# Layer 0 of a two-layer transformer kernel: when x is loaded, where averages and band products are emitted, and where the chain matmuls queue

## The chip, the cores and the metric

The kernel runs on one core of a Trainium2 chip. The metric is device microseconds of one execution. The kernel before took a median of 3630.38 us in three runs (3630.13 to 3631.83).

The engines are named as in the profile: PE is TensorE (matmuls, with weight loads as PEld), DVE is VectorE, ACT is ScalarE, POOL is GpSimd, and SP is SyncE, whose queue issues nearly all DMAs.

## The reference, cut to what matters

The input is `x` of 16 batches x 512 tokens x 128 channels. Layer 0 adds half of a feed-forward network, then an attention, then half of the same network again. Layer 1 (experts around a linear attention) follows; the change doesn't touch it.

```python
x = x + 0.5 * _L0_ffn_ref(_layernorm(x), w_gate, w_up, w_down)
x = x + _L0_attn_ref(_layernorm(x), W_qkv, b_qkv, W_out, b_out, rel_emb_k, rel_emb_v)
x = x + 0.5 * _L0_ffn_ref(_layernorm(x), w_gate, w_up, w_down)

# _L0_ffn_ref: every linear quantizes its input and its weights to FP4 in blocks of 16
h = silu(fp4_linear(x, w_gate)) * fp4_linear(x, w_up)      # 128 -> 352
return fp4_linear(h, w_down)                               # 352 -> 128

# _L0_attn_ref: 16 heads of 8 channels, 512 queries and keys, relative positions clipped at 64
score = einsum('bhqd,bhkd->bhqk', q, k) + einsum('bhqd,qkd->bhqk', q, pe_k)
attn = softmax(score)
ctx = einsum('bhqk,bhkd->bhqd', attn, v) + einsum('bhqk,qkd->bhqd', attn, pe_v)
```

## The kernel before, in words

**Units.** Layer 0 works in 32 units: 16 batches, each in two halves of 256 queries. Unit `u = 2b + h` is half `h` of batch `b`. A unit has eight blocks of 32 queries (`bb`) and four key tiles of 128 (`kt`), so 32 score tiles of 128 keys x 512 (16 heads x 32 queries).

**Scores twice.** A score tile (`scores`, L263 and L267) is 4 matmuls of keys against queries, and 8 more with relative positions where the block lies near the diagonal ("in band"). It goes into one of three PSUM banks (`sps`, pool `pS`). `maxima` makes all 32 tiles of a unit once to find each query's maximum: VectorE reduces each tile (L341), then two reductions (L347), a transpose on TensorE (L349), and a write to DRAM and back (L353, L355) put the negative maximum into a row of the query tile `BD`. `main` makes the same tiles again, with the maximum subtracted; ScalarE takes the exponential (L369) into `PT`, one tile of 128 x 16 x 256 per key tile, in a pool of three buffers.

**Averages and band part.** After the eight scores of a key tile, `main` emits 16 matmuls `av<-PT,a_V` (averages of the values and the sum of weights, in two PSUM banks). After the last key tile that a group of four blocks needs, it emits the products with the relative value embeddings (`rps<-PT,a_TV`, 64 columns each) in two portions of two blocks, and four copies to `RV` (L403). Both go through `run` (L272, L274), which keeps a portion's matmuls together. At the unit's end `RV` goes to DRAM (`RD`, L406) and comes back in another layout as `a_cr` (L409), and ScalarE copies the averages to `cx` (L412).

**The chain around it.** Per batch and half there are `head` (the first feed-forward network, `FFN.half`), `fin` (L422 adds `a_cr` to `cx`; then transposes L430, division, transposes L437, copy L438, output projection L440, residual) and `tail` (the second network and the store of `x`, L486). Per batch there are `prep` (layer norm, query and key projections, split into two 16-bit parts, 22 DMAs to DRAM: `QS`, `QM`, `KSd`) and `prepV` (values, with adds at L321). `loads` reads the DRAM copies into `a_KS` (two buffers), `a_BD` and `a_TQ` (three buffers each, L315, L329, L330). Tiles of `x` have five buffers; `xload` (L475) fills one on SP's queue at the start of the batch's `head`.

**What sets the order.** Each of these is a Python generator, and a `yield` ends a portion. `interleave` gives each generator a number of portions `n` and a window from `f` to `t` in units, and always emits next the portion whose planned time `f + (t-f)*done/n` is least. The window constants are in `W`: before, `fin` of unit u runs at u+1.45 to u+1.9, its tail in the unit after that, `prep` of batch b+2 at 0 to 0.7 of the even unit 2b, and the head of batch b+3 at -0.1 to 1. Maxima run ahead of `main` by one unit less 14 portions; the 17th portion of a unit's maxima emits the loads of the next unit.

The framework then lays out each engine's queue at build time from a simulated timeline: of the instructions that are ready in it, the one emitted first goes next, so a later one may pass an earlier one that isn't ready. On the chip each engine works its queue strictly in this order. `issue_after(ins)` adds an order edge: what is traced inside is queued behind `ins` on the same engine; it doesn't wait for `ins` to finish.

Before the units, a prologue loads the weights, runs the heads of batches 0, 1 and 2, prep of batches 0 and 1, and the maxima of unit 0 with the first 14 portions of those of unit 1.

Of the kernel before, what the change touches and what calls it, by code (L numbers as in the profile page):

```python
# [8 lines left out]
F32 = mybir.dt.float32  # L9
# [16 lines left out]
class K:  # L26
# [23 lines left out]
    def ln_steps(s, xb, out, wk, n):  # L50
# [12 lines left out]
        yield  # L63
    def quant_steps(s, X, wk, P, nb, tag):

# [18 lines left out]
class FFN:  # L84
# [22 lines left out]
    def half(f, xb, half, wk, pp):  # L107
# [7 lines left out]
        for j in range(2): nc.tensor.transpose(ps[:,j*128:(j+1)*128],xq[:,j*128:(j+1)*128],s.ident)  # L115
        xqT=wk.tile([128,256],F32,name="f_x"); nc.scalar.copy(xqT,ps[:,:256]); yield
        h=wk.tile([128,2,I],F32,name="f_h")
        for j in range(2):
            t=h[:,j,:]
            g=pp.tile([128,512],F32,name="mps")  # L120
            nc.tensor.matmul(g[:,:I],xqT[:,j*128:(j+1)*128],f.wguT[:,0,:],start=True,stop=True)
# [3 lines left out]
            nc.tensor.matmul(u[:,:I],xqT[:,j*128:(j+1)*128],f.wguT[:,1,:],start=True,stop=True)  # L125
# [3 lines left out]
        for j in range(2):  # L129
            ps=pp.tile([128,512],F32,name="mps")  # L130
            for c in range(3):
                P=min(128,I-c*128)
                nc.tensor.transpose(ps[:P,c*128:(c+1)*128],hq[:,j,c*128:c*128+P],s.ident)
            hT=wk.tile([128,3,128],F32,name="hT",bufs=1)
            nc.scalar.copy(hT[:,0:2,:],ps[:,:256])
            nc.scalar.copy(hT[:96,2,:],ps[:96,256:384])  # L136
            for c in range(3):
                P=min(128,I-c*128)
                nc.tensor.matmul(ps[:,384:512],hT[:P,c,:],f.wdT[:P,c,:],start=(c==0),stop=(c==2),skip_group_check=True)  # L139
            nc.vector.scalar_tensor_tensor(xh[:,j,:],ps[:,384:512],0.5,xh[:,j,:],ALU.mult,ALU.add); yield  # L140
# [5 lines left out]
class Attn0:  # L146
# [110 lines left out]
    def scores(a, out, kt, half, b, BD, TQ, KS):  # L257
# [4 lines left out]
        for g in range(4):  # L262
            nc.tensor.matmul(o4[:,g],KS[:,sd,g*512+kt*128:g*512+(kt+1)*128],BD[:,g,:,b*32:b*32+32].rearrange("p h (x j) -> p x h j",j=4),start=(g==0),stop=(not ib and g==3),skip_group_check=True)  # L263
        if ib:
            for x in range(8):
                w0=kt*128-blk*32-x+a.OFF
                nc.tensor.matmul(out[:,x*64:x*64+64],a.ET[:,w0:w0+128],TQ[:,:,b*32+4*x:b*32+4*x+4],start=False,stop=(x==7),skip_group_check=True)  # L267

    xnT={}; pend={}; last=None
# [5 lines left out]
    def prep(a, b, xb, wk, pM):  # L275
# [6 lines left out]
        for j in range(4): nc.tensor.transpose(ps[:,j*128:(j+1)*128],xn[:,j,:],a.ident)  # L282
        xnT=a.xnT[b]=wk.tile([128,512],F32,name="xnT",bufs=2); nc.scalar.copy(xnT,ps); yield
        for z in range(2):
            ps=pM.tile([128,512],F32,name="mps")
            nc.tensor.matmul(ps,a.w[:,z*128:(z+1)*128],xnT,start=True,stop=True)
# [18 lines left out]
        nc.tensor.matmul(ps[:32],a.eb.rearrange("p a b -> p (a b)"),q,start=True,stop=True)  # L305
# [26 lines left out]
    def maxima(a, b, half, wk, pS, pM):  # L332
# [13 lines left out]
        for hh in range(2):  # L346
            nc.vector.tensor_reduce(mk[:,hh],mx.rearrange("p k (x s) b -> p s b x k",s=2)[:,hh],axis=AX.X,op=ALU.max)  # L347
        ps=pS.tile([128,512],F32,name="sps")
        nc.tensor.transpose(ps[:,:128],mk.rearrange("p s b x -> p (s b x)"),a.ident)  # L349
# [8 lines left out]
    def main(a, b, half, X, wk, big, pS, pA, pM):  # L358
        s=a.s; nc=a.nc; i=b%2
        u=(2*b+half)%3; BD=a.BD[u]; TQ=a.TQ[u]; KS=a.KS[b%2]; V=a.V[b%2]; RD=a.RD[half]; cr=a.cr[0]  # L360
        av=[pA.tile([128,512],F32,name=f"av{z}") for z in range(2)]
        RV=wk.tile([128,4,4,4,16],F32,name="RV")
        PT=[None]*4
        for kt in range(4):
            pt=big.tile([128,16,256],F32,name="PT"); PT[kt]=pt
            for bb in range(8):
                ps=pS.tile([128,512],F32,name="sps")
                a.scores(ps,kt,half,bb,BD,TQ,KS)
                nc.scalar.activation(pt[:,:,bb*32:bb*32+32].rearrange("p h (x j) -> p x h j",j=4),ps.rearrange("p (x h j) -> p x h j",x=8,j=4),AF.Exp)  # L369
                yield  # L370
            vs=a.vers(kt,half)
            mms=[]
            for z in range(4):
                for cg in range(4):
                    h=z*4+cg
                    o=av[z//2][cg*32:cg*32+32,(z%2)*256:(z%2)*256+256]
                    fs=(kt==0 and z%2==0)
                    mms.append(((o,V[:,2*kt-1+vs,h*9:h*9+32],pt[:,h,:]),dict(start=fs,stop=(kt==3),skip_group_check=True,tile_position=(0,cg*32))))
            a.run(mms)
# [658 lines left out]
```

## Time and profile before

| | |
|---|---|
| median of three runs | 3630.38 us |
| profiled execution | 3633.94 us, its span 3632.2 us |
| PE busy in the span | 2825.0 us (78%) |
| DVE, ACT, POOL busy | 2444.9, 1693.8, 838.9 us |
| mean granted TensorE clock | 0.900 |
| exps of layer 0 (L369) | from 175.5 to 1974.5 us, 1024 of 0.60 us |
| reduces of the maxima (L341) | from 126.4 to 1921.8 us, 1024 of 0.70 us |
| `x` loads (L475) | 16, the last issued at 1569.6 us |

A slice of the page's second part is 90.8 us, a digit is busy tenths. In a list of waits, a line names the engine and line that waited, what ended the wait, the total in us, the number of waits and the longest. In a table of stretches, each engine has its busy us and its instructions in brackets; then come the mean granted clock, the DMA engines' busy share and GB/s.

### The profile page before, as it was taken

The numbers are of one execution on the slowest core, as the hardware profiler recorded it, in microseconds if no ns is written. First come the engines' busy times: TensorE is split into PE (matmuls) and PEld (weight loads), VectorE is DVE, ScalarE is ACT, GpSimd is POOL, SyncE is SP. The second block draws the span as 40 slices with busy tenths as digits, with TensorE's granted clock in tenths as the row PEclk, the third lists the DMA queues.
The fourth block names the chain that finished last, engine by engine and source line by source line (L and its number), as shares of the span: only waits on it lengthen the run. The fifth ranks groups of instructions, "written<-read, shape, count | busy, mean of one in ns | idle before, by whom it ended". The sixth has DMA issues, their size and how long they took to land. (4 is left out here: it accounts for less than half of the span.)

```text
span 3632.2 us, 95259 instructions
## 1 busy us (share of the span) xinstructions
PE 2825.0 (78%) x40077; PEld 2032.3 (56%) x40077; DVE 2444.9 (67%) x6508; ACT 1693.8 (47%) x3391; POOL 838.9 (23%) x789
## 2 busy tenths in 40 slices
PE   5578989889898889888896388873788888878570
PEld 3357777667676677666775244431565555555230
DVE  5568788777887788877773467774546655655356
ACT  3145555545455454545554155533455454445242
POOL 4122222222222222222110222212112211111226
PEclk8799999999999999999998599886899989989785
DMA  3232222321223222222210111104312222121401
GB/s 105 54 91 71 57 53 59 81 63 52 65 65 77 64 50 58 76 74 62 53 33 19 32 33 36 36 33 123 90 54 73 59 63 56 36 62 36 126 17 46
DMA packets 290159, 217.23 MB, mean 60 GB/s; under 512 B 77402, under 2 KB 257476, under 8 KB 289604
## 3 DMA queue, kind: packets, MB, share of 16 engines
q1 hardware_dynamic: 284468, 207.72, 21.6%
q8 instruction: 315, 5.16, 0.6%
q10 hardware_dynamic: 5264, 3.43, 0.4%
q14 instruction: 112, 0.92, 0.1%
HBM read 110.28 MB, written 100.78 MB: 58 GB/s over the span
## 5 line engine op out<-in xcount | busy, mean ns | idle before, releaser
L341 DVE TRANSPOSE_TENSOR_REDUCE mx<-sps 128x16 f32<-128x512 f32 x1024 | 702.5, 701 | 261.7 <-PE sps L263 137.2
L263 PE MATMUL sps<-a_BD,a_KS 128*128 128x128 f16 x8192 | 736.4, 222 | 136.2 <-DVE mx L341 65.6
L369 ACT ACTIVATE PT<-sps 128x512 f32<-128x512 f32 x1024 | 576.4, 599 | 433.8 <-PE sps L267 238.1
L263 PEld LDWEIGHTS <-a_KS 128*128 128x128 f16 x8192 | 546.1, 98 | 296.4 <-issue 260.0
L59 POOL TENSOR_TENSOR ln_rs<-ln_ve,negh 128x4 f32<-128x4 f32 (+1 forms) x192 | 176.9, 930 | 855.1 <-DVE ln_ve L58 760.6
L267 PE MATMUL sps<-a_TQ,a_ET 128*128 128x64 f16 x7168 | 370.3, 195 | 0.0
L721 DVE SCALAR_TENSOR_TENSOR moe<-mps,oh,moe 128x128 f32<-128x128 f32 x896 | 289.8, 341 | 110.7 <-PE mps L719 96.5
L79 POOL TENSOR_TENSOR q_M<-q_y,q_M 128x704 f32<-128x704 f32 (+2 forms) x129 | 157.0, 1218 | 784.6 <-DVE q_y L78 658.6
L719 PE MATMUL mps<-f_W,T 128*128 128x512 f32 x512 | 297.1, 701 | 24.8 <-DVE moe L721 20.0
L267 PEld LDWEIGHTS <-a_ET 128*128 128x128 f16 x7168 | 311.2, 99 | 2.3 <-issue 1.9
L274 PE MATMUL av<-PT,a_V 128*32 128x256 f32 x3840 | 251.9, 387 | 0.0
L894 DVE TENSOR_TENSOR a_at<-pp,a_cm 128x1024 f32<-128x1024 f32 x128 | 154.3, 1214 | 79.6 <-PE pp L892 78.6
L892 PE MATMUL pp<-a_F 64*128 64x128 f32 x2048 | 169.8, 306 | 41.4 <-DVE a_at L894 30.2
L892 PEld LDWEIGHTS pp<-a_F 64*128 64x128 f32 x2048 | 143.3, 206 | 93.0 <-DVE a_at L894 36.9
L719 PEld LDWEIGHTS mps<-f_W,T 128*128 128x128 f32 x512 | 102.7, 222 | 125.0 <-issue 75.3
L274 PEld LDWEIGHTS av<-PT,a_V 128*32 128x32 f32 x3840 | 121.4, 111 | 68.7 <-issue 5.0
L874 ACT ACTIVATE a_F<-pp 128x1024 f32<-128x1024 f32 x128 | 127.0, 1025 | 46.8 <-PE pp L872 40.5
L62 ACT ACTIVATE xn<-xn,ln_mr,ln_rs 128x128 f32<-128x128 f32 x256 | 103.6, 481 | 95.5 <-DVE ln_mr L60 75.2
L274 PE MATMUL rps<-PT,a_TV 128*32 128x64 f32 x6912 | 134.5, 222 | 4.6 <-issue 4.4
L139 PE MATMUL mps<-wdT,hT 128*128 128x128 f32 (+1 forms) x768 | 126.9, 301 | 5.6 <-ACT hT L136 4.0
L673 ACT COPY f_PT<-St 32x512 f32<-32x512 f32 x128 | 78.7, 615 | 106.0 <-DVE St L672 99.9
L872 PE MATMUL pp<-a_QK,a_PK 128*128 128x512 f16 x256 | 82.7, 413 | 54.4 <-DMA a_QK<-a1d 26.6
(342 smaller groups left out, 5330.2 us busy)
## 6 DMA issues: line engine op xcount, KB each, us to landing
QM<-a_HM SPq DMA_DIRECT2D x180, 128.0 KB
a_TQ<-QM SPq DMA_DIRECT2D x120, 192.0 KB
RD<-RV SPq DMA_DIRECT2D x32, 512.0 KB
a_KS<-KSd SPq DMA_DIRECT2D x128, 96.0 KB
a_QK<-a1d SPq DMA_DIRECT2D x128, 96.0 KB
xn<-X SPq DMA_DIRECT2D x32, 256.0 KB
a1d<-a_hi SPq DMA_DIRECT2D x64, 128.0 KB
a_BD<-QS SPq DMA_DIRECT2D x128, 58.0 KB
```

The lines of the kernel that those rows point to most:

```text
L59: nc.gpsimd.tensor_tensor(rs,ve,s.negh[:,:n],ALU.pow); yield
L79: nc.gpsimd.tensor_tensor(M[:P],y[:P],M[:P],ALU.subtract)
L263: nc.tensor.matmul(o4[:,g],KS[:,sd,g*512+kt*128:g*512+(kt+1)*128],BD[:,g,:,b*32:b*32+32].rearrange("p h (x j) -> p x h j",j=4),start=(g==0 ...
L267: nc.tensor.matmul(out[:,x*64:x*64+64],a.ET[:,w0:w0+128],TQ[:,:,b*32+4*x:b*32+4*x+4],start=False,stop=(x==7),skip_group_check=True)
L274: for p,q in mms[1:]: a.nc.tensor.matmul(*p,**q)
L341: with a.s.tc.high_priority(): r=nc.vector.tensor_reduce(mx[:,kt,:,bb],ps.rearrange("p (i c) -> p i c",c=32),axis=AX.X,op=ALU.max,apply_tr ...
L369: nc.scalar.activation(pt[:,:,bb*32:bb*32+32].rearrange("p h (x j) -> p x h j",j=4),ps.rearrange("p (x h j) -> p x h j",x=8,j=4),AF.Exp)
L719: nc.tensor.matmul(ps,yT[:,j*128:(j+1)*128],a.W[:,e2*4:e2*4+4,:],start=True,stop=True)
L721: nc.vector.scalar_tensor_tensor(moe[:,j,:],ps[:,e*128:(e+1)*128],oh[:,j,e2*4+e:e2*4+e+1],moe[:,j,:],ALU.mult,ALU.add)
L874: nc.scalar.activation(f,ps,AF.Relu)
L892: nc.tensor.matmul(ps[:,hh,bs],f[hh*64:hh*64+64,1,bs],f[hh*64:hh*64+64,0,bs],start=True,stop=True)
L894: nc.vector.tensor_tensor(k,ps.rearrange("p h (b q) -> p (h b) q",b=4),a.cm.unsqueeze(1).to_broadcast([128,8,128]),ALU.mult)
```

## The change

- `x` of batches 3 and later is loaded by a generator of its own, `xl`, through ScalarE's queue, with a window 1.4 to 1.3 units ahead of unit 2b where b+2 is the batch; `head` no longer loads.
- Heads run for batch b+2 (`hl` 2 for 3) in the window -1.05 to 0, `prep` at 1.03 to 1.9, `fin` at 0.6 to 1.0; the head of batch 2 leaves the prologue. Windows are cut at 0 below and 0.5 above.
- `main` yields after each score and nowhere else (32 portions for 59). Averages, band portions and copies are put on a list `todo`; after each score's exp one of them is taken off and emitted, so that those of a key tile come among the scores of the next one, and a unit's last ones among the next unit's first scores. What is left at the end is emitted by `rest`.
- `scores` remembers its last matmul in `lastmm`. The matmuls of `half`, `prep` (not `prepV`), `fin` and the transpose in `maxima` are traced inside `gate`, an `issue_after` of it.
- New yields: between `hT` and the down projection (L136/L139), before the transpose in `maxima` (L349), and between `ct` and the output projection (L438/L440).

```diff
+    lastmm=None
+    def gate(s):
+        return s.tc.issue_after(s.lastmm) if s.lastmm is not None else ExitStack()
...
     def half(f, xb, half, wk, pp):
...
-        for j in range(2): nc.tensor.transpose(ps[:,j*128:(j+1)*128],xq[:,j*128:(j+1)*128],s.ident)
+        with s.gate():
+            for j in range(2): nc.tensor.transpose(ps[:,j*128:(j+1)*128],xq[:,j*128:(j+1)*128],s.ident)
...
             hT=wk.tile([128,3,128],F32,name="hT",bufs=1)
             nc.scalar.copy(hT[:,0:2,:],ps[:,:256])
-            nc.scalar.copy(hT[:96,2,:],ps[:96,256:384])
+            nc.scalar.copy(hT[:96,2,:],ps[:96,256:384]); yield
             for c in range(3):
                 P=min(128,I-c*128)
-                nc.tensor.matmul(ps[:,384:512],hT[:P,c,:],f.wdT[:P,c,:],...)
+                with s.gate(): nc.tensor.matmul(ps[:,384:512],hT[:P,c,:],f.wdT[:P,c,:],...)
...
     def scores(a, out, kt, half, b, BD, TQ, KS):
...
+        a.s.lastmm=getattr(r,"ins",r)
...
     def maxima(a, b, half, wk, pS, pM):
...
+        yield
         ps=pS.tile([128,512],F32,name="sps")
-        nc.tensor.transpose(ps[:,:128],mk.rearrange("p s b x -> p (s b x)"),a.ident)
+        with a.s.gate(): nc.tensor.transpose(ps[:,:128],mk.rearrange("p s b x -> p (s b x)"),a.ident)
...
     def main(a, b, half, X, wk, big, pS, pA, pM):
...
+        PT=[None]*4; T={}; vers=a.vers
+        def avrun(kt):
+            if kt==0: T["av"]=[pA.tile([128,512],F32,name=f"av{z}") for z in range(2)]
+            vs=vers(kt,half)
+            mms=[]
+            for z in range(4):
+                for cg in range(4):
+                    h=z*4+cg
+                    o=T["av"][z//2][cg*32:cg*32+32,(z%2)*256:(z%2)*256+256]
+                    fs=(kt==0 and z%2==0)
+                    mms.append(((o,V[:,2*kt-1+vs,h*9:h*9+32],PT[kt][:,h,:]),dict(start=fs,stop=(kt==3),skip_group_check=True,tile_position=(0,cg*32))))
+            a.run(mms)
+        def rvrun(hb, b0, ks):
+            if b0%4==0: T["rps"]=pA.tile([128,512],F32,name="rps"); T["first"]=[True]*4
+            rps=T["rps"]; first=T["first"]
+            mms=[]
+            ok=[(bb,k) for k in reversed(ks) for bb in (b0+1,b0) if a.inband(k,half*8+bb)]
+            for bb,k in ok:
+                blk=half*8+bb
+                for x in range(8):
+                    cg=x%4; col=(bb-hb*4)*128+(x//4)*64
+                    v0=(blk*32-k*128+a.UO)//8-8*vers(k,half)
+                    mms.append(((rps[cg*32:cg*32+32,col:col+64],a.TV[vers(k,half)][:,x,v0:v0+4,:].rearrange("p v d -> p (v d)"),
+                        PT[k][:,:,bb*32+4*x:bb*32+4*x+4]),
+                        dict(start=first[cg],stop=(k==min(q for p,q in ok if p==bb)),skip_group_check=True,tile_position=(0,cg*32))))
+                    first[cg]=False
+            a.run(mms)
+        def rvcopy(hb):
+            if hb==0: T["RV"]=wk.tile([128,4,4,4,16],F32,name="RV")
+            for c in range(4):
+                nc.scalar.copy(T["RV"][:,:,c,:,hb*8:hb*8+8].rearrange("p j z a -> p a z j"),T["rps"].rearrange("p (a z c j) -> p c a z j",a=8,z=4,j=4)[:,c])
+        def end():
+
+            nc.sync.dma_start(RD[:,:4*8*1024].rearrange("x (r f) -> x r f",f=1024),T["RV"])
+            for c in range(4):
+                src=bass.AP(tensor=RD.tensor,offset=RD.offset+c*64,ap=[[1024,8],[8*1024+256,16],[1,64]])
+                nc.sync.dma_start(cr[c*32:c*32+8].rearrange("p (xj f) -> p xj f",f=64),src)
+            cx=wk.tile([128,4,256],F32,name="cx")
+            for zz in range(2):
+                nc.scalar.copy(cx[:,2*zz:2*zz+2,:].rearrange("p z (b j x) -> p (z b) x j",j=4,x=8),T["av"][zz].rearrange("p (y x j) -> p y x j",x=8,j=4))
+            a.pend[b,half]=cx,cr
         for kt in range(4):
             pt=big.tile([128,16,256],F32,name="PT"); PT[kt]=pt
             for bb in range(8):
                 ps=pS.tile([128,512],F32,name="sps")
                 a.scores(ps,kt,half,bb,BD,TQ,KS)
                 nc.scalar.activation(pt[:,:,bb*32:bb*32+32]...,AF.Exp)
+                if a.todo: a.todo.pop(0)()
                 yield
-            a.run(mms)
-            for _ in range(4): yield
+            a.todo.append(lambda kt=kt: avrun(kt))
             for hb in range(2):
                 bl=range(hb*4,hb*4+4)
                 ks=[k for k in range(4) if any(a.inband(k,half*8+x) for x in bl)]
                 if max(ks)!=kt: continue
...
+                a.todo+=[lambda hb=hb,b0=b0,ks=ks: rvrun(hb,b0,ks) for b0 in bl[::2]]+[lambda hb=hb: rvcopy(hb)]
+            if kt==3: a.todo.append(end)
+    def rest(a):
+        while a.todo: a.todo.pop(0)(); yield
...
     def fin(a, b, half, X, wk, pM):
...
-        ct=wk.tile(...); nc.scalar.copy(ct,ps[:,:256])
+        ct=wk.tile(...); nc.scalar.copy(ct,ps[:,:256]); yield
         ps=pM.tile([128,512],F32,name="mps")
-        for t in range(2): nc.tensor.matmul(ps[:,t*128:(t+1)*128],ct[:,t*128:(t+1)*128],a.wo,start=True,stop=True)
+        with s.gate():
+            for t in range(2): nc.tensor.matmul(ps[:,t*128:(t+1)*128],ct[:,t*128:(t+1)*128],a.wo,start=True,stop=True)
...
-        def xload(b):
-            if b in X or b>=nb: return
+        def xload(b, eng=nc.sync):
             t=xk.tile([128,4,128],F32,name="x"); X[b]=t
-            nc.sync.dma_start(t,tok(src,b))
+            eng.dma_start(t,tok(src,b))
+        def xl(b):
+            xload(b,nc.scalar); yield
         def head(b,h):
-            if b<nb: xload(b); yield from F.half(X[b],h,fk,pF)
+            if b<nb: yield from F.half(X[b],h,fk,pF)
...
-        pl,hl=2,3
-        W=dict(part=0,V=(.6,.7),fin=(.45,.9),prep=(0,.7),tail=1.0,head=(-.1,1))
+        pl,hl=2,2
+        W=dict(part=0,V=(.6,.7),fin=(.6,1.0),prep=(1.03,1.9),tail=1.0,head=(-1.05,0))
...
-        loads(1); ffn2(head,1); run(prep(1)); run(part(14)); ffn2(head,2)
-        S=[(part(99999),33*2*nb,W['part'],2*nb+W['part'])]
+        loads(1); ffn2(head,1); run(prep(1)); run(part(14))
+        S=[(part(99999),34*2*nb,W['part'],2*nb+W['part'])]
...
-                def at(g,n,f,t): S.append((g,n,u+f,u+t))
-                at(A.main(b,h,X,wk,big,pS,pA,pM),59,0,1)
+                def at(g,n,f,t): S.append((g,n,max(u+f,0),max(u+t,.5)))
+                at(A.main(b,h,X,wk,big,pS,pA,pM),32,0,1)
...
-                at(A.fin(b,h,X,wk,pM),5,1+fn[0],1+fn[1])
-                at(tail(b,h),21,1+fn[1]+.001,1+fn[1]+tl)
-                if b+hl<nb: at(head(b+hl,h),21,*W['head'])
+                at(A.fin(b,h,X,wk,pM),6,1+fn[0],1+fn[1])
+                at(tail(b,h),23,1+fn[1]+.001,1+fn[1]+tl)
+                if h==0 and 2<b+hl<nb: at(xl(b+hl),1,-1.4,-1.3)
+                if b+hl<nb: at(head(b+hl,h),23,*W['head'])
...
+        S.append((A.rest(),8,2*nb,2*nb+.15))
```

## The prediction

> **What bounds the kernel now.** The change touches layer 0 only, so I read in this order: the page's forty slices (which stretch is bound by what), busy time by stretch, the waits of TensorE in that stretch, the waits of VectorE and of SP's queue, and at last busy time around single stalls.
>
> The slices come first, 90.8 us each:
>
> ```profile
> PE   5578989889898889888896388873788888878570
> DVE  5568788777887788877773467774546655655356
> PEclk8799999999999999999998599886899989989785
> ```
>
> Layer 0 fills the first 22. From slice 4 TensorE is at 8 to 9 tenths with VectorE one digit below it: TensorE is the engine to fill, and VectorE has little to spare. The steady part by itself (20 units), and below it the units that have no head any more:
>
> ```profile
> core 0: us, PE busy (x) PEld busy (x) DVE busy (x) ACT busy (x) POOL busy (x), PEclk, DMA share, GB/s
> 422.30:1579.60 1157.30, 1024.58 (x18242) 809.03 (x18240) 920.09 (x2070) 588.43 (x1300) 277.93 (x260) 0.98 0.25 64
> 1637.10:1797.70 160.60, 145.37 (x2718) 116.19 (x2718) 121.00 (x255) 82.82 (x180) 27.59 (x27) 0.98 0.23 56
> ```
>
> A unit takes 1157.3/20 = 57.9 us, with 51.2 us of matmuls: 6.6 us idle. That idle time, 212 us in 32 units, is all that a new order can win, because the change takes no arithmetic away. How it is spent, in 175 to 1975 us, TensorE's waits first (total, times, longest):
>
> ```profile
> PE sps L263 <- DVE mx L341: 59.1, 72, 9.0
> PE sps L263 <- ACT PT L369: 35.5, 84, 2.6
> PE mps L437 <- DVE a_V L321: 19.8, 12, 1.8
> PE mps L430 <- DVE cx L422: 12.5, 4, 9.9
> PE sps L349 <- DVE mk L347: 12.0, 17, 2.6
> PE mps L440 <- ACT cn L438: 11.4, 9, 1.8
> PE sps L349 <- DVE hq_sc L71: 9.9, 11, 0.9
> ```
>
> Two kinds: a score that waits for one of the three `sps` banks (95 us), and a chain matmul that stands at the head of the queue before its data (98 us, all lines outside L263, L272, L274). Then VectorE's largest wait on a transfer, and two waits of SP's queue:
>
> ```profile
> DVE ln_st L55 <- DMA x<-in_L_attn_x_dram: 45.5, 11, 5.2
> ```
>
> ```profile
> SPq L409 <- DMA RD<-RV: 274.0, 31, 9.6
> SPq L475 <- DMA X<-x: 28.8, 11, 3.4
> ```
>
> The load of `x` waits for the store of the batch whose buffer it takes, SP issues it 2.6 us late, and VectorE stands for it once per batch. What that does to TensorE, in one stall and the stretch behind it:
>
> ```profile
> 758.30:767.50 9.20, 5.31 (x103) 4.09 (x96) 4.04 (x22) 3.18 (x8) 1.36 (x2) 0.86 0.38 99
> 767.50:772.00 4.50, 4.50 (x62) 4.50 (x61) 3.66 (x12) 2.84 (x8) 0.00 (x0) 0.53 0.22 60
> ```
>
> TensorE idles 3.9 of 9.2 us, and afterwards its granted clock is 0.53.
>
> **The change part by part.** The profiled execution took 3633.94 us (span 3632.2), 3.6 us over the median 3630.38; terms are differences, so I apply them to the median.
>
> *x early.* Over the eleven stalls (each from the wait's start to 4 us past its end) the windows sum to 89.3 us with 57.2 us of matmuls: 32.1 us idle. At the steady share of idle time (132.7/1157.3 = 11.5%) 10.3 us would be idle anyway, so 21.8 us are the stall's. In the next 4.4 to 5.6 us the clock was 0.53 to 0.75 in ten of eleven; length times missing clock is 16.0 us behind the stalls and 4.4 us within. Gone with the stalls: 22 + 18 = 40 us (ends 12, if VectorE's idle is only moved to where it falls behind anyway, and 52, all of idle and clock). I take 40, since the new load comes 0.35 unit (20 us) ahead of its head, five times the mean wait of 4.1 us.
>
> A rule to hold against it: the Trainium skill, "DMA: Bandwidth & Descriptors", section "Issuing engines are not separate DMA queues", says that transfers started by different engines share the same DMA engines and that a second issuer saves only the issue time. By it alone the move to ScalarE's queue would bring 13 issues of 0.39 us on SP, none of it on TensorE, and the sum would be 3620. A second rule: "TensorE: Matmul & The Clock Gate", section "HAM oscillation — how this bites in real kernels", has the clock halve after idle gaps over about 3.4 us. The stalls here hold single gaps of 1.8 to 3.9 us, three of the eleven over 3.4, and the clock fell behind ten of them. By the rule alone the clock's share would be 18 x 3/11 = 5 us and the sum 3593.
>
> *The x loads on ScalarE.* 13 issues of 0.3 to 0.76 us (ScalarE's own issues of `a_TQ`, L330): 4 to 10 us, hidden on an engine 51% busy. If the issue is laid out at the first chance, its wait for the store (28.8 us in eleven) stands before exps instead of before SP's work. VectorE's 45.5 us of waiting made 32.1 us of idle TensorE, 0.7 of it; ScalarE has more slack, so half that rate: +10 (0 to +29).
>
> *A yield and a gate before L349, L440 and L139.* One more portion lies between the producer and the matmul. A score tile costs TensorE (715.8 + 360.7 us)/2001 = 0.54 us (rows of L263, L267). L349: 28 waits, 0.54 of each = 15; L440: 11 waits, 6; L139: 2. Gain 23.
>
> *The gate elsewhere* (L115, L121, L125, L133, L282, L286, L305, L430, L437) adds no wait, only a place in TensorE's order: behind the last score emitted. The other 60 of the 98 us are theirs; L437's 22 us come from `prepV`'s adds between `cn` and its transposes, and both stay in the same stretch of odd units. I take 12 of the 60. Behind a gated matmul stand the scores emitted later, and ScalarE's copy and VectorE's quantization wait for it; with 23 portions per unit a chain step has 2.5 us, a score pair takes 1.1 us, so the chain keeps its plan. Ends for both gates together: 0 and 75 of the 98; taken 35.
>
> *Averages and band part by portion.* Same matmuls, now one portion behind each score of the next key tile. The fourth `PT` of a unit reuses a buffer that the band part still reads; exps emitted before that portion hold two of three `sps` banks meanwhile, some 4 us per unit, while TensorE does averages and band. I see up to 1 us per unit lost after it: 0 to +32; taken +10, as the present waits on `PT` are 35.5 us in 32 units without it.
>
> *Heads, prep and fin moved.* Heads and tails cost 8.8 us of VectorE a half (their twelve largest rows, L70 to L140, 509 us over 58 halves); their number per unit stays one and one, prep goes from even to odd units. The 22 dump issues move with it and now end 0.2 to 0.3 unit before the reload; the reload itself (8 `a_KS`, 4 `a_BD`, 4 `a_TQ`) has to wait for the last score of the unit whose buffers it takes, and that score moves from three quarters of the unit to its end. `a_BD` and `a_TQ` took SP 15 us (762.4 to 777.4); they are needed 0.58 unit = 33 us after the unit's start. Then SP does RD (9.7 us to land) and `a_cr`, needed by the add (L422) at 0.6. It fits by a few us: +5 (0 to +70, priced below).
>
> *Start and end.* Head 2 leaves the prologue (18 us of VectorE, which works 24.2 of 25 us from 150 to 175). But head 1's matmuls now queue behind the first maxima's last score: 32 reduces of 0.70 us from 126 us on end at 149, and with the 38 us that head 1 took now (127 to 165) it ends at 187, 22 us later, and maxima 2 waits for the prep behind it. Taken 0, between -18 and +22. The end drains as before.
>
> Sum: -40 + 10 - 35 + 10 + 5 = -50, so 3630 - 50 = 3580 us.
>
> **The rivals.** *(A) The wait moves from `x` to `a_cr`: slower.* The averages' end comes 0.22 to 0.25 unit into the next unit instead of at its start, and SP has the reload ahead of it. Today, in the unit from 1003.7 us, the reload ends at 1010, RD goes out at 1010.1, `a_cr` at 1020.1 to 1021.1 and the add runs at 1028.6 without a wait, 7.5 us behind. After: reload until 0.3 to 0.38, `a_cr` issued at 0.55, the add planned at 0.6, 3 us behind. If VectorE stands there as it stood for `x`, each costs (32.1 + 20.4)/11 = 4.8 us, 15 of them 72 us, and the sum is 3580 - 5 + 72 = 3647; twice as late about 3700. It decides from 3.3 us of TensorE per unit on (15 x 3.3 = 50). For it: SP already waits 9 us per RD and the order laid out at build time came 4 us too early for `x`. Against it: of 64 adds two wait for `a_cr` now (20.7 us).
>
> *(B) Only x pays.* Gates trade one bubble for another, since 95 us of the waits are for banks and no bank is added: 3630 - 40 + 25 = 3615. For it: in units without heads TensorE still idles 9.5% (145.37 of 160.6). Against it: the L349 and L440 waits come at the same place in every second unit.
>
> *(C) No effect.* TensorE at 89% may already be full, matmul ends being modelled: 3630. Against it: the x stalls, where TensorE does 5.3 us in 9.
>
> **How the numbers follow.** Forecast 0.52 (own range 3535 to 3605), A 0.26, B 0.16, C 0.06. A measurement here tells 0.2%, 7 us, from no change. Faster: 0.52 + 0.14 of B = 0.66; same 0.09 (C and the edges of A and B); slower 0.25. The sum's extremes are 3630 - 145 (52 + 75 + 18) and 3630 + 141 (-12 + 29 + 32 + 70 + 22), not all at once; 3525 leaves out 6 in 100 below and 3670 some 13 above (late `a_cr` at its worst).
>
> **What would show it.** Right: the `x` wait of L55 gone, no half-clock stretch once per batch, L349 and L440 waits under 10 us together, units of 55 to 56.5 us. Wrong: waits of L422 on `a_cr`, of L263 on `a_BD` or `a_KS`, ScalarE waiting on `X`, waits on `PT` far over 35 us, or a first unit that starts after 190 us.

## The result and the profile after

The changed kernel takes 3822.16 us (median of four runs, 3814.56 to 3831.60) beside 3630.26 us of the kernel before (four runs, 3623.89 to 3631.83): a ratio of 1.0533, 95% interval 1.0504 to 1.0563. The forecast was 3580, with a range from 3525 to 3670. The profiled execution's span is 3812.8 us, 180.6 us longer than before's.

In the tables below, engine names and columns are as in the sections above; line numbers are now those of the changed kernel: scores L269 and L273, reduces of the maxima L350, exps L417, the head's statistics L55, the load of `x` L491, its store L504, `RD` L404, `a_cr` L407.

The slices of the page, now 95.3 us each:

```profile
PE   5568787778777877887888738884588788888570
DVE  5656686668667866876777447776455555555457
PEclk8888999999999999999999868987799889989785
```

TensorE shows 7 and 8 where it showed 8 and 9, and VectorE fell with it: the time is not work but standing. The steady part by itself, 20 units as before (a unit is 32 exps):

```profile
core 0: us, PE busy (x) PEld busy (x) DVE busy (x) ACT busy (x) POOL busy (x), PEclk, DMA share, GB/s
506.90:1804.10 1297.20, 1030.05 (x18244) 804.15 (x18241) 928.64 (x2071) 598.36 (x1300) 280.99 (x260) 0.93 0.22 57
```

64.9 us per unit for 57.9. TensorE's busy time grew by 5.5 us in 20 units, its idle time by 134.4 (from 132.7 to 267.2). By the starts of the units' first exps, the loss has a pattern: from unit 4 to unit 25 even units take some 70 us, odd ones 59 to 61; before, they took 57 and 58 on average. Most of the loss is therefore something that happens once per batch. Adding up to the last exp, which comes at 2164.4 us instead of 1974.5 (+190): up to unit 0's start -11, unit 0 +32 (94.1 us for 61.9), unit 1 -10, units 2 to 27 +167, the rest +13.

The waits from 175 to 2165 us, TensorE's, then VectorE's, ScalarE's and those of SP's queue:

```profile
PE sps L269 <- ACT PT L417: 226.1, 126, 15.4
PE sps L269 <- DVE mx L350: 89.3, 124, 8.7
PE mps L445 <- DVE cx L436: 20.3, 15, 4.0
PE mps L139 <- POOL q_M L85: 13.3, 2, 12.9
PE sps L269 <- DMA a_BD<-QS: 12.2, 1, 12.2
```

```profile
DVE ln_st L55 <- DMA x<-in_L_attn_x_dram: 176.1, 11, 16.5
```

```profile
ACT PT L417 <- DMA a_cr<-RD: 145.5, 9, 16.7
...
ACT PT L417 <- DMA X<-x: 32.8, 2, 16.5
```

```profile
SPq L407 <- DMA RD<-RV: 284.3, 31, 9.6
```

Three things matter here. VectorE's wait for `x`, which the change was expected to remove, is still there eleven times and four times as long (176.1 us for 45.5). ScalarE now stands eleven times too, 16 us each, in front of an exp. And TensorE waits 226.1 us for that exp, where it waited 35.5. No exp needs `a_cr` or the store `X<-x`: the profile files ScalarE's idle time under the exp that came after it, and names the transfer that ended last. What stood in the queue was the instruction ahead of that exp, the issue of the `x` load.

One such stall in time (unit 14 starts at 1085.7; start, duration, then engine and line; a q marks an engine's own queue, and the bracket is the idle time ahead and what ended it; rows are left out at the dots):

```profile
1085.03 1.09 SPq L339 DMA_DIRECT2D a_TQ<-QM  x1
...
1087.25 3.14 SPq L339 DMA_DIRECT2D a_TQ<-QM  x1
...
1091.50 3.42 SPq L339 DMA_DIRECT2D a_TQ<-QM  x1
...
1093.68 0.29 DVE L146 SCALAR_TENSOR_TENSOR x<-mps,x 128x128 f32<-128x128 f32 x1 [0.38 <-PE mps L145]
...
1095.79 3.37 SPq L339 DMA_DIRECT2D a_TQ<-QM  x1
...
1099.26 0.73 SPq L404 DMA_DIRECT2D RD<-RV  x1
1108.88 0.27 SPq L407 DMA_DIRECT2D a_cr<-RD  x1
1109.24 0.39 SPq L504 DMA_DIRECT2D X<-x  x1
...
1111.32 0.37 ACTq L491 DMA_DIRECT2D x<-in_L_attn_x_dram  x1
1111.74 1.09 ACT L417 ACTIVATE PT<-sps 128x512 f32<-128x512 f32 x2 [15.62 <-DMA a_cr<-RD]
1112.39 0.59 PE L269 MATMUL sps<-a_BD,a_KS 128*128 128x128 f16 x4 [14.39 <-ACT PT L417]
...
1114.32 0.49 DVE L55 BATCH_NORM_STATS2 ln_st<-x 128x6 f32<-128x128 f32 x2 [15.56 <-DMA x<-in_L_attn_x_dram]
```

The tail's last write to the old batch's `x` ends at 1093.97 us. Its store, on SP, goes out at 1109.24, because SP first has to issue the rest of the reload, then `RD`, and then wait 9 us for `RD` before `a_cr`, which stands ahead of the store. The load that takes this buffer waits for the store, and with it all exps behind it on ScalarE; the new batch's statistics wait for the load, and with them all reduces behind them on VectorE. With no exps and no reduces the three score banks stay full. Neither instruction stands where it was planned. ScalarE reached the load 10.4 us into the unit and VectorE the statistics 13.1 us into it (1096.1 and 1098.8); the plan has 0.6 and 0.95 of a unit, some 35 and 55 us. Busy time in the stall and behind it:

```profile
1096.10:1111.70 15.60, 1.45 (x22) 1.07 (x20) 1.82 (x3) 0.03 (x1) 0.00 (x0) 0.61 0.26 78
1111.70:1116.00 4.30, 3.61 (x36) 1.71 (x35) 0.87 (x5) 1.68 (x3) 0.69 (x1) 0.50 0.23 67
```

TensorE works 1.45 of 15.6 us, and then at a clock of 0.50.

### The profile page after: what moved, and what is told of

Its sections match the earlier page's. It is cut to its first block, busy times and chain, and to the rows that moved or that the text cites. A ratio compares the mean times of both kernels' runs of the same rounds, so it can differ in the third digit from the quotient of the medians.

```text
span 3812.8 us, 95107 instructions
## 1 busy us (share of the span) xinstructions
PE 2839.0 (74%) x40077; PEld 2034.1 (53%) x40077; DVE 2456.5 (64%) x6508; ACT 1709.3 (45%) x3391; POOL 843.1 (22%) x789
## 5 line engine op out<-in xcount | busy, mean ns | idle before, releaser
L269 PE MATMUL sps<-a_BD,a_KS 128*128 128x128 f16 x8192 | 752.0, 220 | 381.2 <-ACT PT L417 227.4
L417 ACT ACTIVATE PT<-sps 128x512 f32<-128x512 f32 x1024 | 605.0, 600 | 719.6 <-PE sps L273 275.7
L269 PEld LDWEIGHTS <-a_KS 128*128 128x128 f16 x8192 | 562.0, 97 | 578.4 <-issue 530.1
L350 DVE TRANSPOSE_TENSOR_REDUCE mx<-sps 128x16 f32<-128x512 f32 x1024 | 708.6, 702 | 180.5 <-PE sps L269 87.9
L273 PE MATMUL sps<-a_TQ,a_ET 128*128 128x64 f16 x7168 | 365.1, 193 | 0.0
L273 PEld LDWEIGHTS <-a_ET 128*128 128x128 f16 x7168 | 305.0, 98 | 1.5 <-issue 1.1
L282 PE MATMUL av<-PT,a_V 128*32 128x256 f32 x3840 | 264.0, 401 | 0.0
L55 DVE BATCH_NORM_STATS2 ln_st<-x 128x6 f32<-128x128 f32 x192 | 46.8, 276 | 177.4 <-DMA x<-in_L_attn_x_dram 176.1
## 6 DMA issues: line engine op xcount, KB each, us to landing
QM<-a_HM SPq DMA_DIRECT2D x180, 128.0 KB
a1d<-a_hi SPq DMA_DIRECT2D x64, 128.0 KB
```

The costliest lines, as they stand in the source:

```text
L269: r=nc.tensor.matmul(o4[:,g],KS[:,sd,g*512+kt*128:g*512+(kt+1)*128],BD[:,g,:,b*32:b*32+32].rearrange("p h (x j) -> p x h j",j=4),start=(g= ...
L273: r=nc.tensor.matmul(out[:,x*64:x*64+64],a.ET[:,w0:w0+128],TQ[:,:,b*32+4*x:b*32+4*x+4],start=False,stop=(x==7),skip_group_check=True)
L282: for p,q in mms[1:]: a.nc.tensor.matmul(*p,**q)
L350: with a.s.tc.high_priority(): r=nc.vector.tensor_reduce(mx[:,kt,:,bb],ps.rearrange("p (i c) -> p i c",c=32),axis=AX.X,op=ALU.max,apply_tr ...
```

## The experiments

All times are medians; each ratio is against the kernel before on the same chip.

| | edit | us | ratio, 95% interval |
|---|---|---|---|
| e1 | after, `x` loads on SP's queue | 3826.18 | 1.0548, 1.0518 to 1.0578 |
| e2 | after, `x` stores on GpSimd's queue | 3782.40 | 1.0429, 1.0409 to 1.0450 |
| e3 | after, gate off in the prologue | 3796.11 | 1.0469, 1.0443 to 1.0495 |
| e4 | after, no gate at all | 3715.11 | 1.0246, 1.0226 to 1.0267 |
| e5 | after, head's statistics held to their place | 3794.36 | 1.0433, 1.0395 to 1.0472 |
| e12 | after, `x` load held to its place | 3717.96 | 1.0269, 1.0252 to 1.0287 |
| e6 | after, both held | 3649.27 | 1.0043, 1.0022 to 1.0064 |
| e7 | e6 without gates | 3639.02 | 1.0017, 1.0002 to 1.0031 |
| e8 | e6, prologue as before | 3628.17 | 0.9972, 0.9953 to 0.9991 |
| e10 | e8, averages and band part in blocks as before | 3650.27 | 1.0046, 1.0029 to 1.0062 |
| e9 | before, own `x` load, later head | 3722.80 | 1.0253, 1.0232 to 1.0274 |
| e11 | e9's loads and head, with gates and new yields | 3749.56 | 1.0300, 1.0281 to 1.0318 |

### e1 to e4: which wait, and is it the gates

**e1**, the load back on SP's queue:

```diff
-            xload(b,nc.scalar); yield
+            xload(b); yield
```

> The changed kernel (3822 us), with the x loads of batches 3 and later issued by SP's queue instead of ScalarE's, at the same place. Theory 1 (ScalarE is what blocks: its x load stands 15 us behind the store of the buffer's last batch, the exps stop, the three score banks fill): ScalarE's 15 us waits go, even units fall from 70 to about 59 us, total 3680 (3660 to 3710). Theory 2 (VectorE is what blocks: it stands as long for the late x, 176 us in eleven waits, and SP sends x no earlier): the stalls stay, 3790 or more. Theory 3 (the gates make the tail late and with it the store): no change, 3800 to 3830.

ScalarE's wait is gone, and nothing is won. VectorE's wait stays, and TensorE's idle time changes its name:

```profile
DVE ln_st L55 <- DMA x<-in_L_attn_x_dram: 181.7, 11, 17.2
```

```profile
PE sps L269 <- DVE mx L350: 262.0, 113, 17.3
PE sps L269 <- ACT PT L417: 59.5, 119, 7.5
```

Two engines stood side by side for the same late transfer, and VectorE alone is enough to hold TensorE. So the issue on ScalarE is not by itself the cause; what is late comes before it.

**e2**, the store (L504) issued by GpSimd, so that it doesn't stand behind `RD` and `a_cr` on SP:

```diff
-            nc.sync.dma_start(tok(dst,b)[:,2*h:2*h+2,:], ...)
+            nc.gpsimd.dma_start(tok(dst,b)[:,2*h:2*h+2,:], ...)
```

> The changed kernel, with the tail's store of x issued by GpSimd's queue instead of SP's; the x load stays on ScalarE. Theories 1 and 2 agree here (the store is ready 15 us before SP issues it, since SP stands behind the reload and its 9 us wait for RD): ScalarE's and VectorE's waits shrink from 15 us to under 5, even units about 59 us, total 3670 (3640 to 3700). Theory 3 (the tail itself is late because of the gates): the waits stay, 3790 or more.

It brings 40 us of the 192, at most a third of what was expected: ScalarE's wait falls to 40.4 us in ten, VectorE's only to 135.3 in eleven. The store and the load now go out early, and the load lands late all the same:

```profile
822.13 0.78 POOL L504 DMA_DIRECT2D X<-x  x1
...
826.80 1.01 SPq L404 DMA_DIRECT2D RD<-RV  x1
827.54 0.38 ACTq L491 DMA_DIRECT2D x<-in_L_attn_x_dram  x1
827.97 1.08 ACT L417 ACTIVATE PT<-sps 128x512 f32<-128x512 f32 x2 [3.85 <-DMA X<-x]
...
837.59 1.37 SPq L407 DMA_DIRECT2D a_cr<-RD  x4
837.78 0.49 DVE L55 BATCH_NORM_STATS2 ln_st<-x 128x6 f32<-128x128 f32 x2 [12.23 <-DMA x<-in_L_attn_x_dram]
```

`x` (256 KB) and `RD` (512 KB) are issued 0.7 us apart and both land 10 to 11 us later. In the stall shown above, where `RD` had already landed, the same load took 2.6 us from the end of its issue (1111.7) to the statistics (1114.3); here it took 9.9 (827.9 to 837.8). The Trainium skill, "DMA: Bandwidth & Descriptors", section "Issuing engines are not separate DMA queues", says that transfers from different issuers run interleaved on the same engines; this pair agrees. SP's queue is therefore one part of the lateness, and the place of the load beside `RD` is another; how much each is worth was not separated.

**e3**, the gate only from the units on:

```diff
-        return s.tc.issue_after(s.lastmm) if s.lastmm is not None else ExitStack()
+        return s.tc.issue_after(s.lastmm) if s.on and s.lastmm is not None else ExitStack()
...
+        s.on=True                          # ahead of the units
```

> The changed kernel, with the gate open until the units begin; nothing else. If the first unit's 94 us (62 before) come from head 1 queueing behind the first maxima's last score (its first matmul at 148 us, 55 us of waiting) and so from the late prep and reload: unit 0 falls to about 65 us, total 3792 (3780 to 3805). If they come from head 2, which left the prologue: no more than 5 us.

26 us back (23 by the ratios), and the statistics' wait is untouched (175.6 us in 11). Unit 0 takes 62.7 us instead of 94.1. In the changed kernel ScalarE waits for head 1's first matmul, which is queued behind the first maxima's last score (window 100 to 200 us):

```profile
ACT f_x L121 <- PE mps L120: 58.6, 3, 55.7
```

**e4**, `gate` returns an empty context, so that no matmul has an order edge:

```diff
-        return s.tc.issue_after(s.lastmm) if s.lastmm is not None else ExitStack()
+        return ExitStack()
```

> The changed kernel with no gate anywhere (the new yields stay). Theory 1: the x stall stays, since store and load keep their queues; TensorE's waits of chain matmuls come back from 18 to about 70 us in 20 units (+80 in 32) and the prologue gets its 30 us back: 3820 to 3880. Theory 3 (the gates are what costs): 3620 to 3700.

107 us back, between the two ranges expected, which looks like a verdict on the gates. The waits say otherwise: VectorE's wait for `x` fell to 86.2 us in 11, 7.8 each instead of 16. Without the edges the layout is another one, and the stalls came out half as long in it; what shortened them wasn't traced. Whether gates pay was not to be read from this kernel; e7 asks it where no such stall is left.

### e5, e6, e12: the two instructions held to their places

The framework's layout, not the emission order, fixes where the load and the statistics stand in their queues. Both are emitted 0.6 and 0.95 unit after the buffer is due to come free; but since nothing else holds them they are laid out at the moment at which, in the layout's simulated timeline, the buffer is free and `x` has landed. That timeline isn't on record; the places in the stall above (10.4 and 13.1 us into the unit for a plan of some 35 and 55) and the next three kernels speak for it. These kernels add an order edge that puts the load, the statistics or both behind what was emitted last on their engine. In **e5** only the statistics:

```diff
-            nc.vector.bn_stats(st[:,j,:],xb[:,j,:])
+            with (s.tc.issue_after(s.lastmx) if late and s.units and s.lastmx is not None else ExitStack()):
+                nc.vector.bn_stats(st[:,j,:],xb[:,j,:])
...
+                a.s.lastmx=a.last
```

`lastmx` is the last reduce of the maxima emitted; `late` is set for heads, `units` once the units begin.

> The changed kernel, with the first statistics (L55) of each head in the units queued on VectorE behind the last reduce of the maxima emitted before them, so that they can't be laid out ahead of their planned place; the x load stays as it is. Theory 4 (x isn't late for its plan; the layout pulls both the x load on ScalarE and the head's first statistics on VectorE forward to the moment at which x's buffer comes free in its estimate, and on the chip that is 12 to 15 us later, so that two in-order queues stand): VectorE's 176 us go, ScalarE's wait stays, 3780 to 3830. If VectorE's wait alone decided: 3660 to 3700.

VectorE's wait for `x` is gone, and ScalarE's stays (120.6 us in 8 under `a_cr`, 47.0 in 3 under `X<-x`). Even units still take 71 to 75 us, odd ones 55 (54.5 to 56.3) for 59 to 61. This is the mirror image of e1, with 28 us won (36 by the ratios), all of it in the odd units.

In **e6** the load as well, behind the last exp emitted:

```diff
-            xload(b,nc.scalar); yield
+            with (s.tc.issue_after(s.lastexp) if s.lastexp is not None else ExitStack()): xload(b,nc.scalar)
+            yield
```

> As the kernel before it, and the x load queued on ScalarE behind the last exp emitted before it, so that it too stays at its planned place 0.6 unit after the buffer comes free. Theory 4: both waits under 20 us in all, no half clock once per batch, even units 58 to 60 us, total 3680 (3660 to 3700), the prologue's 30 us still in it. If x is late even for its planned place (transfers too slow beside the reload): 3760 or more.

3649.27 us: 173 us below the changed kernel, or by the ratios 0.049 of 3630 = 178 us. Neither wait for `x` is left in the lists, even units take 58 to 61 us and odd ones 55. In unit 14 the store of `x` still goes out 24 us into the unit (23.5 in the changed kernel), behind the same wait of SP; the load follows it 12 us later, in its planned place, and no engine stands for it. The steady part (20 units), and TensorE's waits from 175 us to the last exp:

```profile
488.70:1638.70 1150.00, 1029.90 (x18242) 812.31 (x18241) 935.95 (x2071) 598.89 (x1301) 280.86 (x260) 0.98 0.25 64
```

```profile
PE sps L271 <- DVE mx L352: 73.1, 116, 8.8
PE sps L271 <- ACT PT L420: 65.8, 79, 7.9
PE mps L449 <- DVE cx L440: 20.3, 15, 3.8
```

The same busy time in 1150 us for 1297, and the clock back at 0.98.

**e12** is the missing corner, the load alone:

```diff
-            xload(b,nc.scalar); yield
+            with (s.tc.issue_after(s.lastexp) if s.lastexp is not None else ExitStack()): xload(b,nc.scalar)
+            yield
```

> Only the x load on ScalarE's queue is put behind the last exp emitted; the head's first statistics stay where the layout puts them. Theory 1 (the two waits stand beside each other, each enough to hold TensorE): ScalarE's wait on X goes, and so does most of its wait on RD-late exps; VectorE's wait on x stays or grows, since its statistics are still laid out by the estimate and the load now comes later than the layout's estimate had it only if that estimate was wrong: 3760 to 3830 us, even units 68 to 72. Theory 2 (the layout puts the statistics where it thinks the load lands, so a load in its place takes the statistics along): VectorE's waits on x fall under 60 us in eleven, even units 58 to 63, 3640 to 3690 us.

3717.96 us, between the two numbers expected. The waits went as the second theory said: ScalarE's wait for the store is gone, and VectorE's is nearly so, because the layout now expects `x` later and moves the statistics with it.

```profile
DVE ln_st L56 <- DMA x<-in_L_attn_x_dram: 19.2, 12, 2.7
```

The time did not go all the way. In unit 14 the load goes out 36 us into the unit, as in e6, but the statistics follow at 42 us where e6 has them at 55 (1057.9), and even and odd units both come out 2 to 4 us longer on average than in e6 (59 to 65 and 57 to 62 us), with TensorE's waits for banks at 102.9 and 88.7 us for 73.1 and 65.8. So a head ahead of its plan costs time even when it waits for next to nothing. The odd units, which hold no stall, tell the two apart: with gates and portions in and the statistics free they take 57 to 62 us (the changed kernel, e1, e2, e3, e12), with the statistics held 55 (e5, e6, e8). What the early head does to TensorE there wasn't traced further.

The four corners by ratio: neither 1.0533, statistics 1.0433, load 1.0269, both 1.0043. Holding the statistics alone wins 36 us, holding the load alone 96, both together 178. That is more than the sum, and two waits that cover each other are only part of the reason: holding the load already takes both waits away. The 82 us between e12 and e6 come from putting the head in its place. In this order some 96 of the 178 us are the price of the waits and 82 that of an early head; in the other order, e5 first, 36 go to the head and 142 to the wait that is left.

### e7, e8, e10: the other parts of the change, where no stall hides them

**e7** is e6 without any gate:

```diff
-        return s.tc.issue_after(s.lastmm) if s.lastmm is not None else ExitStack()
+        return ExitStack()
```

> As the kernel before it, without the gates on TensorE. If gates gain what TensorE's waits say (chain waits 18 us in 20 units with them, some 70 without): the units lose 80 us, the prologue gains 26, 3735 against 3680. If gates cost (the ungated change was 107 us faster): 3600 to 3660.

**e8** is e6 with the gate off in the prologue (the edit of e3) and the head of batch 2 back in it:

```diff
-        loads(1); ffn2(head,1); run(prep(1)); run(part(14))
+        loads(1); ffn2(head,1); run(prep(1)); run(part(14)); ffn2(head,2)
...
-                if b+hl<nb: at(head(b+hl,h),23,*W['head'])
+                if 2<b+hl<nb: at(head(b+hl,h),23,*W['head'])
```

> Head and x load in place and gates as in the kernel two before, with the prologue as before the change (no gate in it, head 2 in it). Theory 4 and the prologue's gate add up: 3680 - 30 = 3650 (3620 to 3670), unit 0 at 62 us. A total under 3625 would beat the kernel before the change.

e8 is 21.1 us faster than e6 on the same chip, and it is the one kernel faster than before, by 0.3%: 0.9972, 0.9953 to 0.9991. e7, without any gate, is 10.3 us faster than e6, which is inside the range expected if gates cost; but it has rid the prologue of its gate too. Taking the gate from the prologue alone is worth 21 us (e6 to e8, with head 2 moved along) to 26 us (e3), so the gates inside the units earn the difference, 11 to 16 us, if the two effects add. The new yields stay in all these kernels, so they are not measured.

**e10** is e8 with the old `main`: averages and band part in blocks after their key tile, 59 portions:

```diff
-            a.todo.append(lambda kt=kt: avrun(kt))
+            mms=[]
+            for z in range(4):
+                for cg in range(4):
...
+            a.run(mms)
+            for _ in range(4): yield
```

> The last kernel of the round before (3628 us: head and x load in place, gates, prologue as before) with the averages and the band part emitted as before the change, in a block behind the eight scores of their key tile. There all waits for x are gone and the gates are worth some 11 us, and yet it gains 8 us only. If the portions behind single scores cost the rest (exps that hold score banks until the band part is through): 3575 to 3605. If the moved windows (prep in odd units, fin later) cost it: 3615 to 3640.

Slower than either range expected: 3650.27 us beside e8's 3628.17, with the kernel before at 3635.79 and 3635.70 on the two chips: one portion behind each score is worth about 22 us, by the ratios 27. TensorE's waits up to 1980 us, about the end of layer 0's exps, in e10 and then in e8, which have the same line numbers here except for the exp:

```profile
PE sps L271 <- DVE mx L352: 94.9, 123, 8.6
PE sps L271 <- ACT PT L382: 33.3, 80, 0.8
PE mps L141 <- DVE qklo L318: 21.5, 12, 3.2
...
PE mps L141 <- POOL q_M L87: 7.6, 10, 1.0
```

```profile
PE sps L271 <- DVE mx L352: 74.6, 122, 8.7
PE sps L271 <- ACT PT L420: 69.1, 77, 9.6
PE mps L449 <- DVE cx L440: 20.6, 15, 4.1
...
PE mps L141 <- DVE qklo L318: 2.4, 2, 1.6
```

With the portions the waits for an exp double; those for a reduce and at the transposes of L141 fall by more, and the last exp comes 13.5 us earlier (1976.6 for 1990.1). The gain is larger in the full units and partly lost at the end: from the start of unit 4 to that of unit 26 the portions are 27 us faster (1263.1 us for 1290.1), in units 28 to 31, which have no heads, 15 us slower (190 for 175).

### e9 and e11: the load of x alone, on the kernel before

**e9** gives the kernel before a load of its own ahead of the head, still on SP, and moves the head later and its statistics behind the last reduce:

```diff
+        def xl(b):
+            xload(b); yield
...
-        W=dict(part=0,V=(.6,.7),fin=(.45,.9),prep=(0,.7),tail=1.0,head=(-.1,1))
+        W=dict(part=0,V=(.6,.7),fin=(.45,.9),prep=(0,.7),tail=1.0,head=(.15,1.1))
...
+                if h==0 and b+hl<nb: at(xl(b+hl),1,-.1,0)
```

> The kernel before (3630 us) with one thing changed: x is loaded by SP at its present place, and the head starts a quarter of a unit later, its first statistics queued behind the last reduce emitted, so that VectorE never stands for x. The prediction's x term alone: 3590 (12 to 52 us faster). If the eleven stalls only hide idle time that falls elsewhere anyway: 3618 to 3635.

It did not isolate the `x` term, because it did not remove the wait:

```profile
DVE ln_st L57 <- DMA x<-in_L_attn_x_dram: 128.0, 11, 12.6
```

128.0 us for 45.5, and 87 us slower than before on the same chip (3722.80 for 3635.79; 92 by the ratio). Nor did the load stay in its present place. Before, it went out some 10 us ahead of the even unit; here it goes out 12 to 14 us into it, because SP issues the store only behind the whole reload, then `RD`, then the load (804.33, 805.11 and 809.19 us in unit 10, whose reload ends at 804.2). A planned quarter of a unit was no lead here.

**e11** has the same load and head on before's windows, `main` and prologue, with the gates and the new yields in the units:

```diff
+        return s.tc.issue_after(s.lastmm) if s.on and s.lastmm is not None else ExitStack()
...
+            with s.gate(): nc.tensor.matmul(g[:,:I], ...)
...
-            nc.scalar.copy(hT[:96,2,:],ps[:96,256:384])
+            nc.scalar.copy(hT[:96,2,:],ps[:96,256:384]); yield
```

> The kernel before with x in place as in the first of this round, and the gates and new yields of the change in the units only; averages, windows of prep and fin, and prologue as before. The prediction's x and gate terms together: 3630 - 40 - 35 = 3555; with the gates at the 11 us that their run showed: 3580. If the gates only trade one bubble for another: no faster than the first of this round.

The stall grew again (144.5 us in 11, longest 14.5), so this run tells nothing of gates by themselves. Both miss what was expected of them. What an undisturbed `x` is worth on the kernel before stays unmeasured.

## Why the prediction was wrong

**x early, -40: the step that failed.** It read: "I take 40, since the new load comes 0.35 unit (20 us) ahead of its head, five times the mean wait of 4.1 us." It took the distance between two planned windows for a distance between two instructions in queues. On the chip there was no lead: the head's statistics were laid out as soon as `x` was expected to land, whatever the windows said (e12 moves the load, and the statistics move with it; in the changed kernel they stand 13 us into the unit for a plan of some 55). And the moment itself was taken from before, where SP issued the store between two pieces of the `a_KS` reload (756.3 us in the stall shown there) and the load 3.9 us later; in the new order the tail ends while SP has `a_BD`, `a_TQ`, `RD` and the 9 us wait ahead of the store, which goes out 15 us late. VectorE's wait went from 45.5 to 176.1 us instead of to none. (The 18 us for the clock in the sum of this term stand beside 16.0 + 4.4 = 20.4 without the step between them; nothing hangs on it.)

**The x loads on ScalarE, +10 (0 to +29): right mechanism, wrong size.** "If the issue is laid out at the first chance, its wait for the store stands before exps" is what happened. The price was worked out from the 28.8 us that SP waited for the store before; the wait is now 178.3 us (145.5 + 32.8). Both terms together came out at +178 by e6 instead of -30; in the order e12, e6 that is some 96 for the waits and 82 for a head ahead of its plan, which no term had. A rule that bears on it was at hand: the Trainium skill, "DMA: Bandwidth & Descriptors", section "Anatomy of one DMA — SWDGE (gpsimd) path", says that the DMA engines themselves don't wait for semaphores, and that such a wait is spent on the sequencer that issues the transfer, before dispatch. ScalarE's 15.62 us of standing at the issue of `x` agree with it.

**Heads, prep and fin moved, +5 (0 to +70): the place was right, the victim wasn't.** The prediction had SP full after the reload, with a fit "by a few us", and rival A made the late `a_cr` the wait that decides. The add on `a_cr` waited only 16.3 us in 2 (20.7 in 2 before). What SP's lateness delayed was the store of `x` behind it. The prediction listed SP's work up to `a_cr` and didn't ask what is queued behind that wait. So rival A had the sign and the queue, not the wait.

**Yields and gates, -35 (0 to 75): right in what goes; the gates bring less than forecast.** The waits of L349 and L440 (33.3 us) are gone from the list, and TensorE's waits at chain matmuls fell from 98 to 51 us; 34 of the 51 are L445's for `cx` and two of L139 for GpSimd. In time the gates are worth 11 to 16 us in the units; the yields, part of the term's 23 us for L349, L440 and L139, were never taken out alone. Waits for banks took over part of the idle time, as rival B argued: 138.9 us in e6 for 104.1 in e7, which has no gates.

**Averages and band part by portion, +10 (0 to +32): wrong sign.** The term was a cost of up to 1 us per unit; measured, the portions earn 22 to 27 us in all (e10). The feared cost exists (waits for an exp 69.1 us for 33.3), but the blocks cost more in waits for reduces and at L141 (124.0 us for 77.4).

**Start and end, 0 (-18 to +22): the mechanism was named, the size missed.** "Head 1's matmuls now queue behind the first maxima's last score" is the 55.7 us wait of `f_x`; it was set off in full against the head that left the prologue. Measured, the gate in the prologue costs 23 to 26 us (e3). "The end drains as before" did not hold either: units 28 to 31 take 190 us for 177, and 175 with the old blocks (e10), so this is the portions' doing.

**Where the hoped-for gain is now.** With both stalls gone and the prologue as before (e8) the sum is -10 us by the ratio (-8 by the medians), of which portions and gates account for -33 to -43. If the parts add, the rest of the change, `x` and the yields and all that was moved, still costs some 23 to 33 us, where the forecast had -25 (-40, +10 and +5). The profile of e8 shows what stands there now, once in every even unit (58 to 62 us; odd ones 54.7). ScalarE's copies to the single `RV` buffer wait until its last contents have gone out to `RD`, a transfer that SP issues behind the reload:

```profile
763.95 3.30 SPq L341 DMA_DIRECT2D a_TQ<-QM  x1
...
767.34 0.97 SPq L407 DMA_DIRECT2D RD<-RV  x1
...
777.68 1.01 ACT L404 COPY RV<-rps 128x128 f32<-128x128 f32 x4 [4.87 <-DMA RD<-RV]
...
779.17 0.39 PE L271 MATMUL sps<-a_BD,a_KS 128*128 128x128 f16 x4 [3.15 <-ACT PT L420]
```

```profile
ACT RV L404 <- DMA RD<-RV: 68.6, 14, 10.7
```

21.1 us in 9 before. This is read from the trace; a kernel with the reload or `RD` in another place wasn't tried.

**The signs it named.** Of the signs of being wrong, "ScalarE waiting on `X`" and "waits on `PT` far over 35 us" both came. The first unit started at 164 us, not after 190, but took 94.1. L349 and L440 fell under 10 us, as it said for the right case; units of 55 us did not come in this kernel, and with both stalls gone only in every second unit (the odd ones in e6 and e8, the even ones in e7).

## What to carry to other kernels

A planned window says when an instruction is emitted, not where it ends up in its engine's queue: where the layout is free to pull an instruction forward that waits for a transfer, hold it with an order edge behind the work that it must not stop, above all a DMA issue on an engine that computes. Before moving a load, follow the whole chain that frees its buffer (last write, store, the queue of the store and what that queue waits for) in the new order, not in the old profile. When two engines stand for the same late transfer, taking one wait away may show little (nothing in e1, 36 us in e5); take both, and each alone, before calling either harmless. And look at the stretches without a stall too: here they showed that the early head cost time by itself.

## What the runs showed of the hardware

- An issue on SP isn't a fixed price. In the reload the first `a_TQ<-QM` (192 KB) took SP 1.09 us and the later three 3.14 to 3.42, while the DMA engines were busy 22 to 35% of the time; what makes them long wasn't tested. SP's own time for the reload's last part was thus 14 us (1085.0 to 1099.2).
- The load of 256 KB of `x` took 2.6 us from the end of its issue with `RD` landed, and 9.9 us when issued 0.7 us after `RD`'s 512 KB (e2).
- Behind an idle gap of 14.39 us the granted clock was 0.50 over 4.3 us, and the mean of the steady part fell from 0.98 to 0.93. The Trainium skill, "TensorE: Matmul & The Clock Gate", section "HAM oscillation — how this bites in real kernels", has the clock fall after gaps over some 3.4 us; these long gaps agree with it and don't test the bound.
